# Two more input blocks through GpSimd's queue, and the last part of w turned earlier to make room for a fourth output buffer

## The chip, the cores and the metric

The kernel runs on one core of one Trainium2 chip. The metric is the device time of one execution in microseconds (us); of a kernel that was run several times the median is given. Below, DMA stands for the transfers between the chip's main memory (HBM) and the core's on-chip memory, which the core's 16 DMA engines carry out. TensorE, VectorE, ScalarE, GpSimd and SyncE are the core's engines; the profile calls them PE (with PEld for its weight loads), DVE, ACT, POOL and SP.

## The reference

For every pair of fields (i, j) with i < j, the vector of field i is multiplied by that pair's own 64 x 64 matrix, and the result is multiplied element by element with the vector of field j. There are 4096 rows, 32 fields of 64 numbers, and 496 pairs.

```python
r_inputs   # (4096, 32, 64) float32
L0_rec_W   # (496, 64, 64) float32

def _L0_rec_ref(inputs, W):
    F = inputs.shape[1]
    idx_i, idx_j = np.triu_indices(F, k=1)
    vi = inputs[:, idx_i, :]
    vj = inputs[:, idx_j, :]
    vidots = jnp.einsum('bpd,pde->bpe', vi, W)
    return vidots * vj          # (4096, 496, 64) float32
```

The input is 33.6 MB, the matrices are 8.1 MB, and the output is 520 MB.

## The kernel before

**Tiles and blocks.** The 4096 rows are cut into 16 blocks of 256 rows, and a block into 2 tiles of 128 rows, one row on each of the 128 partitions: 32 tiles, numbered 0 to 31. A block of the input is loaded as a whole (2 MB). The on-chip array `xb` has five slots of one tile each. Slots 1 to 4 hold the first two blocks; `slots_of` (line 103) says which two slots each later block takes.

**The steps.** For one tile, the work is a list of steps, each for one field i and up to 16 fields j. A step is two matmuls (line 305, the two halves of the 64 outputs), which write one PSUM tile, and an element-wise product with the fields j (line 321, VectorE), which writes the output buffer. For seven fields i (`aside`) the first step's PSUM tile is instead copied by ScalarE (line 318) and multiplied by GpSimd (line 319). Before a tile's fields can be used by TensorE, they are transposed eight at a time (`turn_x`: four transposes on TensorE, three copies on ScalarE).

**Outputs.** The steps of a tile are gathered in groups. In tiles 0 to 2 there are six groups, and these three tiles go side by side: group 0 of tiles 0, 1, 2, then group 1 of tiles 0, 1, 2, and so on. That makes 18 outputs, numbered 0 to 17 here (in places 0 to 137 of the whole order of steps; group 3 fills places 54 to 77). From tile 3 on a tile has four groups and 47 steps, and the tiles follow one another. A group fills one of three output buffers in the array `ob` (`out_home`, line 79), which SyncE then sends to HBM as one transfer of 2.3 to 4.1 MB (line 326). A buffer is written again only when its transfer has landed, that is, when all 16 DMA engines have finished their share.

**The matrices.** w is loaded in four parts (`load_w`). A part is raw at first, and must be reordered (`order_w`, line 179) and transposed (`turn_w`, line 190: 8 transposes on TensorE and a copy for each of four quarters). Parts 1 to 3 are ordered and turned in between the first steps, at the places in the list at line 248. The raw form of the last part lies at the end of `ob`, behind the three small buffers of the first three tiles.

**Reloading x.** At step 4 of tiles 3, 7, 11, 15, 19, 23 and 27, two blocks are loaded for the four tiles that come next (`loads`, line 257). A block in the list `fifteen` goes by `load_fifteen` (line 151) on GpSimd's own DMA queue, as four transfers: 120 rows, which fifteen of the DMA engines share; a tiny one (`turn_engines`) whose data nobody uses, and which moves on the engine at which the next transfer begins; and the last 8 rows in two halves, one to eight engines each. Any other block goes by `load_x` on ScalarE's queue, three steps later, as one transfer of 128 rows shared by all 16 engines. Before the change the odd block of each pair goes by GpSimd, the even one by ScalarE; of the last pair, 14 and 15, both go by GpSimd.

**What sets the order.** Each engine runs its own instructions in the program's order. The issues of GpSimd's transfers stand among its multiplies (line 319), and those of ScalarE among its copies. SyncE issues the outputs alone. Loads and outputs share the same 16 DMA engines.

Of the kernel before, what the change touches and what calls it, by code (L numbers as in the profile page):

```python
# [12 lines left out]
def kernel(  # L13
# [39 lines left out]
    LEAD = 3  # L53
    lead = [0, p0[3], p0[6], p0[9], p0[13], p0[18], NP]
    later = [0, p0[4], p0[9], p0[15] + 10, NP]
    groups = {}
# [3 lines left out]
    cap0 = max(b - a for a, b in groups[0])  # L60
    cap1 = max(b - a for a, b in groups[LEAD])
# [14 lines left out]

    def out_home(n: int, later_: bool):
        o, c = ((2 - n % 3) * cap1, cap1) if later_ else ((2 - n % 3) * cap0, cap0)  # L80
        return ob[:, o : o + c, :]

    RAW, RP = P * E2 // D, 2 * BANK // D
    assert 3 * cap0 + RAW + 2 * RP <= 3 * cap1 and LEAD * len(groups[0]) % 3 == 0

# [10 lines left out]

    fifteen = (3, 5, 7, 9, 11, 13, 14, 15)

    def slots_of(blk: int):
        e, second = divmod(blk, 2)
# [64 lines left out]
    def raw_w(c: int):  # L169
        if c + 1 < len(wrows):  # L170
            a = wrows[c + 1][0]
            return wT[:, a : a + P, :].rearrange("p r e -> p (r e)")
        return ob[:, 3 * cap1 - RAW :, :].rearrange("p r e -> p (r e)")
# [5 lines left out]
    def order_w(c: int, k: int, copy):  # L179

        r = wrows[c][1] - wrows[c][0]
        o = k * RP if c == 0 else 3 * cap1 - RAW - (1 + k % 2) * RP
        rp = ob[:, o : o + RP, :].rearrange("p r e -> p (r e)").rearrange("p (e h d) -> p e h d", h=2, d=D)
        src = raw_w(c)[:r].rearrange("p (d h e) -> p e h d", h=2, d=D)
        ins = copy(rp[:r], src[:, k * EU : (k + 1) * EU])  # L185
        if c > 0:
            tc.keep_in_program_order(ins)
        return rp
# [59 lines left out]
    for c, orders, turns in (  # L248
        (1, (2, 4, 8, 10), (4, 7, 12, 15)),
        (2, (16, 18, 26, 29), (24, 27, 32, 36)),  # L250
        (3, (56, 58, 66, 72), (62, 68, 74, 78)),
    ):
        for k in range(NU):
            due.setdefault(orders[k], []).append(("order", c, k))
            due.setdefault(turns[k], []).append(("turn", c, k))
# [15 lines left out]
    for k, copy in enumerate((v, v, v, a)):  # L271
        rps[0, k] = order_w(0, k, copy)
# [6 lines left out]
    for s, (t, st) in enumerate(sched):  # L279
# [8 lines left out]
        for what, *args in due.get(s, ()):  # L288
            if what == "x":
                xT[tuple(args)] = turn_x(*args, a)  # L290
            elif what == "turn":
                turn_w(*args, rps.pop(tuple(args)), a)
            else:
                c, k = args
                rps[c, k] = order_w(c, k, ((v, v, p, v), (v, v, p, a))[k % 2][c])
# [3 lines left out]
        if pa == base:  # L299
            ot = out_home(len(n_out), t >= LEAD)  # L300
            n_out[t, g] = ot
# [10 lines left out]
        o = pa - base  # L312
# [45 lines left out]
```

## Time and profile before

| | |
|---|---|
| median of 4 runs | 1330.44 us (1328.27 to 1330.67) |
| profiled execution: its time | 1328.27 us |
| profiled execution: its span | 1326.5 us |
| busy: TensorE / VectorE / ScalarE / GpSimd | 1138.7 / 950.2 / 471.4 / 561.9 us |
| bytes moved | 563.17 MB, mean 425 GB/s |
| read / written in HBM | 41.94 / 520.09 MB |
| output transfer of 3.8 to 4.1 MB, issue to landing | 19.5 to 20.2 us (median) |
| block by ScalarE's queue (6 of them), issue to landing | 22.6 us (median) |
| 120 rows of a block by GpSimd's queue (8 of them), issue to landing | 33.5 us (median) |

The span is the time from the first to the last instruction of the profiled execution; its device time is 1.8 us more. The slices of the page cut the span into 40 equal parts. Their row "DMA" is the busy share of the 16 DMA engines in tenths, and their row "GB/s" what was moved. In the rows of queues, q1 is SyncE's queue, q10 ScalarE's, and q0 GpSimd's, each with its packets, its MB and the time of its packets as a share of 16 engines' span. In an answer by windows a row begins with the stretch (from:to in us) and its length; then come the busy us of PE, PEld, DVE, ACT and POOL with the number of instructions, the granted clock of TensorE, the share of the DMA engines and the GB/s. A row of the timeline is: start in us, length in us, engine, line, operation, and how many instructions were merged.

The trace also has a record of every completion: a transfer adds one to its semaphore for each of the 16 DMA engines, so the sixteen times say how far apart the engines finish, though not which engine is which.

### The profile page before, as it was taken

The numbers are of one execution on the slowest core, as the hardware profiler recorded it, in microseconds if no ns is written. First come the engines' busy times: TensorE is split into PE (matmuls) and PEld (weight loads), VectorE is DVE, ScalarE is ACT, GpSimd is POOL, SyncE is SP. The second block draws the span as 40 slices with busy tenths as digits, with TensorE's granted clock in tenths as the row PEclk, the third lists the DMA queues.
The fourth block names the chain that finished last, engine by engine and source line by source line (L and its number), as shares of the span: only waits on it lengthen the run. The fifth ranks groups of instructions, "written<-read, shape, count | busy, mean of one in ns | idle before, by whom it ended". The sixth has DMA issues, their size and how long they took to land.

```text
span 1326.5 us, 17383 instructions
## 1 busy us (share of the span) xinstructions
PE 1138.7 (86%) x6644; PEld 595.4 (45%) x6644; DVE 950.2 (72%) x1287; ACT 471.4 (36%) x627; POOL 561.9 (42%) x268
## 2 busy tenths in 40 slices
PE   6989978997998978999788987889889989878883
PEld 4545544443444434444344444444444444444441
DVE  5668777784777857777677776777767777667773
ACT  4453423332333333333233332333323333333330
POOL 1862524435343444344443353443524435334440
PEclk9999989997999989999899998999989999989997
DMA  9999999999999999999999999999999999999999
GB/s 387 431 431 429 384 431 433 428 430 423 432 429 432 433 418 432 431 430 433 413 431 434 429 425 421 432 429 431 412 423 434 431 429 397 421 430 431 434 431 389
DMA packets 24658, 563.17 MB, mean 425 GB/s; under 512 B 3456, under 2 KB 3456, under 8 KB 3840
## 3 DMA queue, kind: packets, MB, share of 16 engines
q1 hardware_dynamic: 20448, 532.69, 93.9%
q0 software_dynamic: 3264, 16.80, 3.4%
q10 hardware_dynamic: 864, 12.58, 2.4%
q8 instruction: 52, 0.85, 0.2%
q14 instruction: 30, 0.25, 0.0%
HBM read 41.94 MB, written 520.09 MB: 424 GB/s over the span
## 4 chain that ended last, share of the span: by engine, by line
DMA 52%; PE 19%; DVE 10%; issue 9%; POOL 5%; ACT 3%; DVEq 0%; ACTq 0%; SPq 0%; POOLq 0%
DMA out_dram<-ob 51%; PE ps L305 17%; DVE ob L321 10%; POOL ob L319 4%; ACT ob L318 3%; PE ptx L204 1%; DMA xb<-in_r_inputs_dram 1%; POOL xb L156 0%; DVE ob L185 0%; ACT xtb L206 0%; ACT xtb L208 0%; ACT xtb L207 0%; POOL ob L185 0%; POOL scratch L148 0%; DVEq L321 0%
## 5 line engine op out<-in xcount | busy, mean ns | idle before, releaser
L321 DVE TENSOR_TENSOR ob<-ps,xb 128x1024 f32<-128x1024 f32 (+4 forms) x1277 | 940.2, 793 | 343.6 <-DMA out_dram<-ob 181.9
L305 PE MATMUL ps<-wT,xtb 64*128 64x512 f32 (+15 forms) x5760 | 1010.5, 488 | 151.3 <-DVE ob L321 76.6
L319 POOL TENSOR_TENSOR ob<-ob,xb 128x1024 f32<-128x1024 f32 x224 | 529.8, 2371 | 735.0 <-ACT ob L318 716.9
L305 PEld LDWEIGHTS ps<-wT,xtb 64*128 64x128 f32 x5760 | 504.9, 194 | 620.2 <-DVE ob L321 258.1
L318 ACT COPY ob<-ps 128x1024 f32<-128x1024 f32 x224 | 226.8, 1013 | 484.9 <-PE ps L305 307.9
L206 ACT COPY xtb<-ptx 128x512 f32<-128x512 f32 x122 | 71.5, 586 | 306.5 <-PE ptx L204 304.8
L204 PE MATMUL ptx<-ident,xb 128*128 128x128 f32 x512 | 84.8, 289 | 2.2
L204 PEld LDWEIGHTS ptx<-ident,xb 128*128 128x128 f32 x512 | 54.4, 142 | 54.3 <-issue 33.2
L208 ACT COPY xtb<-ptx 64x512 f32<-64x512 f32 x122 | 71.0, 582 | 3.0
L207 ACT COPY xtb<-ptx 64x512 f32<-64x512 f32 x122 | 70.5, 577 | 3.0
L305 PE MATMUL ps<-wT,xb 64*128 64x512 f32 (+15 forms) x244 | 41.5, 461 | 3.0 <-ACT ob L318 1.6
L305 PEld LDWEIGHTS ps<-wT,xb 64*128 64x128 f32 x244 | 20.6, 186 | 19.9 <-DVE ob L321 6.6
L195 PE MATMUL ptw<-ident,ob 128*128 128x128 f32 (+1 forms) x128 | 18.8, 299 | 10.8 <-DVE ob L185 10.2
L195 PEld LDWEIGHTS ptw<-ident,ob 128*128 128x128 f32 (+1 forms) x128 | 15.7, 158 | 15.9 <-issue 12.4
L196 ACT COPY wT<-ptw 128x1024 f32<-128x1024 f32 (+1 forms) x15 | 14.9, 992 | 9.8 <-PE ptw L195 9.8
L156 POOL DMA_DIRECT2D xb<-in_r_inputs_dram x24 | 15.2, 635 | 0.0
L185 DVE COPY ob<-wT 128x1024 f32<-128x1024 f32 (+1 forms) x7 | 7.1, 1041 | 8.8 <-DMA wT<-in_L_rec_W_dram 8.8
L148 POOL DMA_DIRECT2D scratch<-in_r_inputs_dram x10 | 9.2, 916 | 0.3 <-issue 0.3
L206 ACT COPY xb<-ptx 128x512 f32<-128x512 f32 x6 | 3.5, 588 | 13.4 <-PE ptx L204 13.3
L185 POOL COPY ob<-wT 128x1024 f32<-128x1024 f32 x4 | 7.9, 1984 | 0.0
L185 ACT COPY ob<-wT 112x1024 f32<-112x1024 f32 x1 | 2.0, 1965 | 6.7 <-DMA wT<-in_L_rec_W_dram 6.7
L185 ACT COPY ob<-ob 128x1024 f32<-128x1024 f32 x2 | 4.0, 2019 | 0.0
(11 smaller groups left out, 12.8 us busy)
## 6 DMA issues: line engine op xcount, KB each, us to landing
out_dram<-ob SPq DMA_DIRECT2D x29, 4064.0 KB, 19.5
out_dram<-ob SPq DMA_DIRECT2D x29, 4032.0 KB, 19.9
out_dram<-ob SPq DMA_DIRECT2D x29, 4000.0 KB, 20.0
out_dram<-ob SPq DMA_DIRECT2D x29, 3776.0 KB, 20.2
xb<-in_r_inputs_dram POOLq DMA_DIRECT2D x8, 1920.0 KB, 33.5
xb<-in_r_inputs_dram ACTq DMA_DIRECT2D x6, 2048.0 KB, 22.6
out_dram<-ob SPq DMA_DIRECT2D x3, 2912.0 KB, 12.6
out_dram<-ob SPq DMA_DIRECT2D x3, 2624.0 KB, 11.3
```

The lines of the kernel that those rows point to most:

```text
L156: tc.keep_in_program_order(nc.gpsimd.dma_start(out=dst[ps, :, fs], in_=rows[ps, :, fs]))
L185: ins = copy(rp[:r], src[:, k * EU : (k + 1) * EU])
L195: nc.tensor.transpose(pt[:, n, :r], rp[:r, n].rearrange("p h d -> p (h d)"), ident[:r, :r])
L196: copy(wT[:, a:b, k * EU : (k + 1) * EU], pt[:, :, :r].rearrange("p e r -> p r e"))
L204: nc.tensor.transpose(pt[:, u, :], x_tile(t)[:, f : f + 2, :].rearrange("p f d -> p (f d)"), ident)
L206: copy(xT[:, 0], pt)
L207: copy(xT[D:, 1], pt[:D])
L208: copy(xT[:D, 1], pt[D:])
L305: nc.tensor.matmul(ps[:, h, :m, :], xT[t, i // RUN][h * D : (h + 1) * D, (i + h) % 2, i % RUN // 2, :], wT[h * D : (h + 1) * D, pa : pa + ...
L318: nc.scalar.copy(dst, src)
L319: nc.gpsimd.tensor_mul(dst, dst, xj)
L321: nc.vector.tensor_mul(dst, src, xj)
```

## The change

Three edits. The blocks 6 and 10 are put into `fifteen`, so that they go by GpSimd's queue too, in four transfers; by `slots_of` their blocks and the blocks 7 and 11 take other slots. The last part of w is ordered at places 40 to 52, not 56 to 72, and turned at places 46 to 58, not 62 to 78. The memory that its raw form leaves is a fourth output buffer for the last eight of the 18 outputs of the first three tiles (from output 10 on, in place 62); the first ten go round three buffers, in another order than before. The reordered form of w's first part moves behind the first buffer.

```diff
+    FOURTH = 3 * len(groups[0]) - 8
+
     def out_home(n: int, later_: bool):
-        o, c = ((2 - n % 3) * cap1, cap1) if later_ else ((2 - n % 3) * cap0, cap0)
+        if later_:
+            o, c = (2 - n % 3) * cap1, cap1
+        elif n < FOURTH:
+            o, c = (0, 2, 1)[n % 3] * cap0, cap0
+        else:
+            k = 3 - (n - FOURTH) % 4
+            o, c = k * cap0 if k < 3 else 3 * cap1 - cap0, cap0
         return ob[:, o : o + c, :]

     RAW, RP = P * E2 // D, 2 * BANK // D
-    assert 3 * cap0 + RAW + 2 * RP <= 3 * cap1 and LEAD * len(groups[0]) % 3 == 0
+    assert 3 * cap0 + RAW + 2 * RP <= 3 * cap1 and LEAD == 3 and FOURTH % 3 == 1
...
-    fifteen = (3, 5, 7, 9, 11, 13, 14, 15)
+    fifteen = (3, 5, 6, 7, 9, 10, 11, 13, 14, 15)
...
-        o = k * RP if c == 0 else 3 * cap1 - RAW - (1 + k % 2) * RP
+        o = cap0 + k * RP if c == 0 else 3 * cap1 - RAW - (1 + k % 2) * RP
...
-        (3, (56, 58, 66, 72), (62, 68, 74, 78)),
+        (3, (40, 42, 48, 52), (46, 50, 54, 58)),
```

## The prediction

> **What bounds the kernel now.** I read the slices of the page first, then the queues, the seven places where x is reloaded, and last who was late there.
>
> Slices and queues of the page:
>
> ```profile
> DMA  9999999999999999999999999999999999999999
> GB/s 387 431 431 429 384 431 433 428 430 423 432 429 432 433 418 432 431 430 433 413 431 434 429 425 421 432 429 431 412 423 434 431 429 397 421 430 431 434 431 389
> ...
> q1 hardware_dynamic: 20448, 532.69, 93.9%
> q0 software_dynamic: 3264, 16.80, 3.4%
> q10 hardware_dynamic: 864, 12.58, 2.4%
> ```
>
> The DMA engines are never free. At the plateau of 433 GB/s the 563.17 MB take 1300.6 us of the 1326.5. So the bound is transfer, and only stretches below the plateau can be won. They are the start, the end, and the reloads. The same from windows laid over the reloads (R1 at 145 us to R7 at 1115) and one plateau (last column GB/s):
>
> ```profile
> 138.00:148.00 10.00, 9.89 (x56) 5.15 (x58) 8.86 (x12) 2.77 (x5) 5.50 (x6) 1.00 0.94 374
> 148.00:158.00 10.00, 9.93 (x65) 5.57 (x62) 8.09 (x12) 5.11 (x6) 9.73 (x5) 1.00 1.03 342
> 158.00:180.00 22.00, 15.47 (x93) 8.80 (x91) 13.01 (x20) 6.25 (x10) 4.07 (x2) 0.84 1.01 426
> 200.00:240.00 40.00, 36.93 (x216) 19.08 (x218) 31.45 (x44) 15.18 (x21) 18.08 (x8) 0.96 1.01 433
> 299.00:340.00 41.00, 31.43 (x168) 16.02 (x164) 23.85 (x33) 12.83 (x18) 17.65 (x11) 0.83 1.00 423
> 462.00:503.00 41.00, 31.88 (x178) 17.04 (x174) 24.71 (x35) 13.05 (x18) 17.90 (x11) 0.88 1.01 421
> 626.00:667.00 41.00, 31.74 (x188) 16.43 (x186) 25.74 (x38) 13.06 (x18) 17.86 (x11) 0.92 1.00 416
> 788.00:829.00 41.00, 30.24 (x178) 15.41 (x174) 24.58 (x35) 13.06 (x18) 17.69 (x11) 0.92 1.00 416
> 952.00:993.00 41.00, 32.12 (x180) 17.09 (x178) 24.68 (x36) 13.06 (x18) 17.24 (x11) 0.83 1.01 411
> 1114.00:1155.00 41.00, 35.12 (x200) 18.39 (x196) 27.52 (x40) 14.06 (x19) 21.70 (x16) 0.92 1.00 393
> ```
>
> Loss = (433 - rate)/433 x length. R1: 1.36 + 2.10 + 0.36 = 3.8 us; R2 0.95; R3 1.1; R4 1.6; R5 1.6; R6 2.1; R7 3.8. Sum 15.0 us: all that this change can touch.
>
> Why the losses grow from R2 to R7 is in the trace's completion records, sixteen increments for each transfer, one per DMA engine. On the plateau one engine ends each output transfer about 0.33 us further behind the median of the sixteen than in the transfer before. Its lag at the last output before the reload's packets is 1.5 us at R2, 4.1 (R3), 5.3 (R4), 6.4 (R5), 8.2 (R6), 6.6 (R7). A reload whose second block goes by GpSimd's queue takes some 4 to 5 us off; R7, with both blocks there, turned +6.6 into -5.3. An output buffer comes free with the last engine, so the lag delays the next output. The first engine finished an output this long before the next was issued or, positive, after it: +6.8 us ahead of R2, +4.0 (R3), +2.4 (R4), +2.8 (R5), +1.5 (R6), +1.6 (R7). I call it the backlog. When it is used up, engines hold loads alone, and those go at 250 to 300 GB/s (8 KB load packets 478 ns in R7's worst 20 us, 309 ns when mixed with outputs).
>
> Last, GpSimd in R7, where it issues both blocks as it would in R3 and R5, and in R3 as it is now:
>
> ```profile
> 1114.62 0.79 POOL L156 DMA_DIRECT2D xb<-in_r_inputs_dram  x1
> 1115.40 0.98 POOL L148 DMA_DIRECT2D scratch<-in_r_inputs_dram  x1
> 1116.38 1.87 POOL L156 DMA_DIRECT2D xb<-in_r_inputs_dram  x3
> 1118.25 0.96 POOL L148 DMA_DIRECT2D scratch<-in_r_inputs_dram  x1
> 1119.21 1.11 POOL L156 DMA_DIRECT2D xb<-in_r_inputs_dram  x2
> 1120.34 4.66 POOL L319 TENSOR_TENSOR ob<-ob,xb 128x1024 f32<-128x1024 f32 x2
> ```
>
> ```profile
> 462.89 0.79 POOL L156 DMA_DIRECT2D xb<-in_r_inputs_dram  x1
> ...
> 465.79 2.35 POOL L319 TENSOR_TENSOR ob<-ob,xb 128x1024 f32<-128x1024 f32 x1
> ```
>
> The multiply behind the issues is the last work of the tile's first output. In R3 it ends at 468.14 and SP issues the output at 468.17; in R7 the first multiply ends at 1122.7, the output goes at 1122.73.
>
> **The change part by part**
>
> *Blocks 6 and 10 leave ScalarE's queue (R3, R5).* Removed: one issue of 0.38 us on ScalarE, three steps later in the program; nobody waits for it. Added on GpSimd: four issues, 5.72 us (1114.62 to 1120.34) in place of 2.9 (462.89 to 465.79), so the multiply and the output behind it come 2.8 us later; SP has nothing else to issue meanwhile. Without a ScalarE load between them the output packets ahead also finish sooner: the output ahead of R7 ended 10.7 us after its forerunner on the first engine, that of R3 13.7, that of R5 12.4. R3: the first engine ended 6.6 us after the next issue; 6.6 - 2.8 - 3.0 = 0.8, and by the median engine 10.6 - 2.8 - 4.3 = 3.5. In R7 these were -1.6 and +0.5 for a loss of 3.8, in R6 2.9 and 5.4 for 2.1. In R7 most engines ran out of outputs, here half would. I take 2.0 us for R3, +0.9 (bounds 0 and R7's own 3.8, +2.7). R5: 4.2 - 2.8 - 1.7 + 4 (lag, below) = 3.7, nearest to R4's 4.4: loss 1.3, -0.3 (bounds -0.7 and +2.2).
>
> *Bytes for the other fifteen engines.* A block by GpSimd gives fifteen engines 16 packets of 8 KB (309 ns) and two of 4 KB (159 ns), 5.26 us; by ScalarE's queue 8 packets of 16 KB (611 ns), 4.89. Two blocks: +0.75 us. The page's queue shares, which hold the slow reloads too, give 6.0 against 5.3: +1.4 is the other end. The lagging engine finishes some 1.6 us ahead already, so what it is spared at the end is worth nothing.
>
> *The lag.* R3's pair takes off about 9.7 in place of 4.5, R5's as well, against 5.3 grown between reloads. By this count it is 4.1 at R3, near 0 at R4, 1 at R5, and ahead of the others from then on. What is late next is the spread of the other fifteen, about 2 us. The backlog then returns to R2's 6.8. R4: 1.6 to 1.0, -0.6 (0 to -0.7). R6: 2.1 to 1.0, -1.1 (0 to -1.2). R7: -1.6 + 5.2 = 3.6, its double issue stays; 3.8 to 1.4, -2.4 (0 to -2.9). The lower ends are R2's loss, the upper ends no effect.
>
> *The last part of w and the fourth buffer (R1).* Four orders (VectorE 1.03 and 1.56 us, ScalarE 2.00 and 2.04), four turns (TensorE 1.09 each, ScalarE copies 1.01 each) stand between 79.6 and 98.3 us. From 79.1 to 140 VectorE never waits for an output buffer, and TensorE is busy 9.4 to 10 of each 10 us from 80 to 120: the stage is bound by TensorE. Places 40 to 52 for orders and 46, 50 for two turns fall in the outputs at 66 to 78 us, where VectorE waited 1.4 and 1.2 us for buffers: that covers 2.2 us on TensorE; without it these outputs would slip, with a backlog of 4.5 us there. The turns at 54 and 58 stay in the bound stage. So the outputs up to the first of tile 3 come 2.2 us earlier (0 if the stage is set by other waits, 4.4 if all turns count). That first output was issued at 150.11, 2.6 us after the first engine was out of outputs (147.50); then 147.9. Its loads move up with it and stretch the output ahead. The loss of 0.6 us at 139 goes, and of the later dip about a third: -1.6 (bounds +0.5, a slip of the early outputs; and -2.8, R2's level). The fourth buffer itself allows more lead than the bound stage can use: 0. New output homes are only addresses, and the first tile-3 output still waits for the same transfer (135.84).
>
> *A rule against this change.* The trace's lag grows 0.33 us per output between 350 and 450 us, where GpSimd moves nothing. The Trainium skill, "DMA: Bandwidth & Descriptors", section "Latency and other measured facts", guesses that two slower engines are slow because of GpSimd's descriptor rings, and calls this specific to its path. By that, two more blocks there would feed the lag: R4 to R7 would keep their losses and the sum would be near 1330.5. The rows above are against it.
>
> Sum: +0.9 - 0.3 + 0.75 - 0.6 - 1.1 - 2.4 - 1.6 = -4.35 us, of a span of 1326.5 to 1322.2. The profiled execution was 1328.27, the lowest of four and 2.2 below their median; I carry the difference to the median: 1330.44 - 4.35 = **1326.1**.
>
> **Rivals**
>
> *The dips are reads beside writes, not lag.* For it: R2 loses 0.95 with hardly any lag. Against: R6 and R7 lose twice to four times as much. Then R4, R5, R6 keep theirs, R7 wins half (-1.2), R1 -1.0, R3 +0.9, bytes +0.75: -0.55, 1329.9.
>
> *Slower: the double issue on GpSimd makes R7's dip.* For it: R7 had less lag than R6 and lost 1.7 more, and its output waited for that multiply. Then R3 and R5 go to 3.8 (+2.7, +2.2), R7 stays, R4 and R6 win 1.7, R1 1.6, bytes +0.75: +2.35, 1332.8. It decides once the output behind the issues comes after the median engine has finished the one ahead (R7: 0.5 us of margin); I expect 3.5 in R3.
>
> *All at R2's level.* R1 -2.8, R4 -0.7, R5 -0.7, R6 -1.2, R7 -2.9, R3 0, bytes +0.75: -7.55, 1322.9. Against it is the double issue.
>
> **How the numbers follow.** Forecast 0.45 (own range 1324 to 1328), reads 0.25, double issue 0.17, R2's level 0.13. What a measurement of this kernel can tell from no change is about 0.2%, 2.7 us: faster below 1327.8. Faster: 0.13 + 0.40 of the forecast + 0.02 of the reads = 0.55; slower 0.15 + 0.03 of the reads = 0.18; same 0.27. The range reaches to both outer cases: 1322 to 1333.
>
> **What the changed profile would show.** Right: ScalarE's queue moves 8.39 MB and GpSimd's 20.99; R4, R6 and R7 at 420 GB/s or more; R3 near 412; the lagging engine ahead of the others at the end by some 10 us; no w order or turn after 80 us, and tile 3's first output near 148. Wrong: R6 and R7 unchanged though the lag is gone, or R3 and R5 below 400, or the early outputs late by more than 4.5 us.

## The result, and the profile after

The changed kernel takes 1332.4 us (median of 36 runs, 1329.04 to 1334.93), the kernel before 1330.2 us in the runs beside it (56 runs, 1327.94 to 1332.06). The ratio is 1.0016, with a 95% interval of 1.0011 to 1.0021: about 2 us slower, where 4.35 us less were forecast. The profiled execution took 1330.38 us, with a span of 1328.6; it is among the quicker ones of this kernel, and 2.1 us above that of before.

Slices and queues of the page of the changed kernel:

```profile
GB/s 388 434 428 433 396 432 431 431 430 427 431 430 432 430 410 427 431 429 420 423 431 432 431 422 420 425 430 429 416 424 433 429 434 403 426 432 429 431 433 352
...
q1 hardware_dynamic: 20448, 532.69, 93.9%
q0 software_dynamic: 4064, 21.00, 4.1%
q10 hardware_dynamic: 576, 8.39, 1.6%
q8 instruction: 52, 0.85, 0.2%
```

GpSimd's queue has two blocks more, ScalarE's two less, as it should be. The slice of the first reload rose from 384 to 396, that of the last from 397 to 403. The last slice of all fell from 389 to 352: 37/433 of 33.2 us, or 2.8 us, are lost there, at the end, where the prediction put nothing.

The same windows over the reloads as in the prediction, with two added right behind R3 and R5 (503 to 530 and 829 to 856 us), for the changed kernel (last column GB/s):

```profile
138.00:148.00 10.00, 9.93 (x54) 4.91 (x54) 9.09 (x11) 4.78 (x6) 8.31 (x7) 1.00 0.98 388
148.00:158.00 10.00, 6.31 (x40) 3.68 (x40) 5.27 (x9) 2.52 (x3) 5.80 (x3) 0.95 1.01 365
158.00:180.00 22.00, 20.11 (x122) 10.17 (x122) 15.23 (x25) 7.31 (x12) 5.23 (x3) 0.95 1.02 431
299.00:340.00 41.00, 31.15 (x172) 16.01 (x170) 23.33 (x34) 12.04 (x17) 16.23 (x10) 0.83 1.00 425
462.00:503.00 41.00, 33.32 (x198) 17.01 (x196) 27.68 (x40) 13.57 (x19) 20.14 (x15) 0.96 1.00 412
503.00:530.00 27.00, 19.30 (x97) 10.07 (x95) 14.16 (x18) 7.59 (x10) 13.44 (x6) 0.87 1.01 428
626.00:667.00 41.00, 30.02 (x174) 15.31 (x175) 23.55 (x35) 12.05 (x17) 15.15 (x8) 0.88 1.01 417
788.00:829.00 41.00, 32.29 (x186) 17.25 (x185) 26.50 (x37) 13.05 (x18) 18.29 (x13) 0.92 1.00 415
829.00:856.00 27.00, 20.85 (x104) 10.85 (x100) 14.56 (x19) 8.26 (x11) 13.59 (x6) 0.81 1.01 424
952.00:993.00 41.00, 28.73 (x168) 14.71 (x168) 23.09 (x34) 12.05 (x17) 14.78 (x8) 0.88 1.01 417
1114.00:1155.00 41.00, 31.20 (x184) 17.23 (x182) 25.50 (x37) 12.04 (x17) 18.68 (x13) 0.92 0.99 405
```

By the prediction's own formula the losses are now R1 2.7, R2 0.8, R3 2.0, R4 1.5, R5 1.7, R6 1.5, R7 2.7 us, 12.8 in place of 15.0. Behind R3 and R5 the two added windows had 431 and 430 GB/s before: 0.2 and 0.4 us more are lost there. So the reloads gave back 1.6 us of time, and the kernel still ended 2 us later.

The trace's completion records say how both can be. The lines below are the sixteen times at which the engines finished one output, each less their median, in us; in front stand the number of the output (by transfers: the very first output goes as two, so the last of the 135 is 134) and the time of its issue.

```
before
118  1150.0  -5.3  -0.9  -0.5  -0.4  -0.4  -0.2  -0.2  -0.0   0.0   0.0   0.1   0.2   0.3   0.3   0.3   0.8
134  1306.4  -1.6  -1.3  -1.2  -1.1  -0.6  -0.4  -0.4  -0.2   0.2   0.5   0.6   0.7   0.7   0.7   0.9   1.0
changed
118  1152.7  -3.6  -2.1  -1.4  -1.0  -0.9  -0.6  -0.4  -0.1   0.1   0.4   0.4   0.6   1.2   1.3   2.0   3.1
134  1308.5  -3.2  -1.8  -1.8  -1.1  -1.0  -0.7  -0.1  -0.1   0.1   0.4   0.5   0.5   0.6   1.6   1.9   3.8
```

Before the change the last output left the mean engine at 1324.26 us and the last one 1.08 us after it. In the changed kernel the mean engine ends at 1323.53, so 0.73 us earlier, and the last one 3.79 us behind it, at 1327.32. -0.73 + 2.71 = +2.0 us, of the 2.1 us by which the spans differ. A second profile of the changed kernel (below) has the last engine 3.88 us behind, 2.8 more than before, and the mean engine 0.4 us later than before, not earlier. In the packet records one engine works alone for the last 1.9 us: two packets of 32,256 bytes, 1.194 us each, the second behind the first, when all others have ended before the middle of the first.

That engine is not the slow one of the prediction. The slow engine shows in the packet records by its longer packets: between 350 and 450 us, before and after the change, one packet in sixteen or seventeen takes 1,207 to 1,255 ns, nearly all others 1,194; that is about 0.04 us more each, and eight such packets in an output make some 0.3 us. Followed by these packets it was 6.4 us late ahead of R7 before the change and 4.5 early behind it (output 120); in the changed kernel 3.2 late and 3.3 early, and level with the median at output 132. The engine that ends last is one of the other fifteen, and it was 3.1 us behind as R7's reload went through (output 118). The second profile shows the same with four engines, 2.9 to 4.4 us behind there and 3.5 to 4.6 at the end:

```
changed, second profile
118  1153.1  -3.7  -1.6  -0.9  -0.9  -0.7  -0.7  -0.5  -0.3   0.3   0.4   0.6   0.6   2.9   3.7   3.7   4.4
134  1309.7  -2.0  -1.8  -1.8  -0.9  -0.8  -0.6  -0.3  -0.1   0.1   1.0   1.1   1.6   3.5   4.1   4.1   4.6
```

### The profile page after: what moved, and what is told of

Same layout as the page of the kernel before. It is cut to its first block, busy times and chain, and to the rows that moved or that the text cites. A ratio compares the mean times of both kernels' runs of the same rounds, so it can differ in the third digit from the quotient of the medians.

```text
span 1328.6 us, 17395 instructions
## 1 busy us (share of the span) xinstructions
PE 1137.5 (86%) x6644; PEld 596.5 (45%) x6644; DVE 951.4 (72%) x1287; ACT 471.5 (35%) x627; POOL 566.6 (43%) x276
## 5 line engine op out<-in xcount | busy, mean ns | idle before, releaser
L165 POOL DMA_DIRECT2D xb<-in_r_inputs_dram x30 | 18.9, 633 | 0.0
```

What stands on the lines that cost most here:

```text
L165: tc.keep_in_program_order(nc.gpsimd.dma_start(out=dst[ps, :, fs], in_=rows[ps, :, fs]))
```

## The experiments

The theories change as the runs come in. Theory A: the last engine sets the end, and what a kernel leaves of the spread between the engines decides. Theory B, the prediction's own way of counting: the sum of the stretches' losses sets it, so that the loss sits in the double issue of R3 and R5. Later ones are named where they come up: the state theory is A made narrower (what counts is how R7 leaves the engines), the count theory holds the number of split blocks against it.

All times are medians; the ratios are to the kernel before on the same chip. "Split" means a block by `load_fifteen`. The last three columns come from the profiled execution of each kernel: R7's rate, by how much the last engine is behind the median at output 118, and the last output's mean engine and last engine.

| kernel | split blocks | time, us | ratio (95% interval) | R7, GB/s | last at 118 | mean end + last behind it |
|---|---|---|---|---|---|---|
| before | 8 | 1330.2 | 1 | 393 | 0.8 | 1324.3 + 1.1 |
| changed | 10 | 1332.4 | 1.0016 (1.0011 to 1.0021) | 405 | 3.1 | 1323.5 + 3.8 |
| changed, again | 10 | 1332.1 | 1.0021 (1.0012 to 1.0029) | 414 | 4.4 | 1324.7 + 3.9 |
| blocks only | 10 | 1331.36 | 1.0013 (1.0004 to 1.0021) | 418 | 3.9 | 1324.5 + 3.4 |
| w and buffer only | 8 | 1328.91 | 0.9996 (0.9987 to 1.0004) | 391 | 2.2 | 1323.6 + 1.3 |
| second block late | 10 | 1333.25 | 1.0023 (1.0012 to 1.0035) | 418 | 3.0 | 1326.1 + 3.3 |
| 6 and 10 whole | 8 | 1329.22 | 0.9994 (0.9985 to 1.0003) | 396 | 1.0 | 1323.7 + 1.2 |
| 6 and 10 whole, again | 8 | 1329.97 | 1.0003 (0.9994 to 1.0013) | 390 | 1.0 | 1323.8 + 1.4 |

**The two parts alone.** The first run has only the edit of `fifteen`, the second only the other two edits.

```diff
-    fifteen = (3, 5, 7, 9, 11, 13, 14, 15)
+    fifteen = (3, 5, 6, 7, 9, 10, 11, 13, 14, 15)
```

> Of the three edits only blocks 6 and 10 by GpSimd's queue; w and the output buffers as before. The profile after the change gave, against before: R1 to R7 lost 2.2 us less in all, but the last engine ended 3.8 us behind the median of the sixteen at the last output, where before it was 1.0. Theory A (the end is set by the one engine that is last; what the reloads save on the average engine is given back in a wider spread at the end): +3 us against before, and a spread of 3 to 4 us at the end. Theory B (the double issue on GpSimd, which holds up a multiply and the output behind it, is the whole cost): R3 and R5 lose about 1 us more each, +1.5 us, spread at the end as before. If the whole +2.2 us lies in the early w and the buffers: within 0.5 us of before.

```diff
+    FOURTH = 3 * len(groups[0]) - 8
...
+        elif n < FOURTH:
+            o, c = (0, 2, 1)[n % 3] * cap0, cap0
...
-        (3, (56, 58, 66, 72), (62, 68, 74, 78)),
+        (3, (40, 42, 48, 52), (46, 50, 54, 58)),
```

> Only the early w and the fourth buffer; blocks 6 and 10 by ScalarE's queue as before. Both theories: the loss at R1 falls from 3.8 us to about 2.7, as in the changed kernel, R2 to R7 as before, spread at the end about 1 us: -1.1 us (0 to -1.6). If this part is what made the change slower: +1 us or more, with the first outputs of group 3 late.

The blocks alone cost 0.13%, the early w and the fourth buffer by themselves can't be told from no change (0.04% less). So the loss comes with the two blocks. The first run doesn't decide between the theories: its 1.5 us are theory B's figure, and R3 and R5 did fall, to 407 and 409 GB/s; the spread at the end is theory A's. Where the blocks are split, the last engine ends 3.4 us behind the mean; without them 1.3.

**Is it the double issue on GpSimd?** The second block of a pair was issued three steps later, behind the multiply that the output waits for.

```diff
-            for b in (loads[s], loads[s] + 1):
-                if b in fifteen:
-                    load_fifteen(b)
+            load_fifteen(loads[s] + (loads[s] not in fifteen))
+        if s - 3 in loads and loads[s - 3] in fifteen:
+            load_fifteen(loads[s - 3] + 1)
```

> The changed kernel, but where both blocks of a reload go by GpSimd (R3, R5, R7), the second is issued three steps later, behind the multiply that the double issue held up. Theory B: the output behind it goes 2.8 us earlier, R3, R5 and R7 come back to 418 GB/s or more from 412, 415 and 405, and the time falls 2.5 us against the changed kernel. Theory A: the rates come back as well, but the time falls by less than 1 us, since the last engine's lag of 3.8 us at the end stays or grows.

R3's output goes at 468.0 us again, as before the change (468.2; 469.8 with the double issue), and the time does not follow: 1333.25. What the second issue costs the multiply is not what makes the kernel slower. The rates say less: R3 has 420 GB/s, R7 418 and R5 414, but the changed kernel's own second profile has 422, 414 and 414 there, with the double issue in place:

```profile
462.00:503.00 41.00, 30.90 (x188) 16.63 (x186) 26.23 (x38) 12.72 (x19) 19.30 (x14) 0.96 1.00 422
1114.00:1155.00 41.00, 32.92 (x182) 17.58 (x180) 24.87 (x37) 12.04 (x17) 18.87 (x13) 0.88 1.00 414
```

**Is it GpSimd's queue, or the split?** Blocks 6 and 10 stay on GpSimd's queue, but as one transfer of 128 rows over all sixteen engines.

```diff
-                if b in fifteen:
+                if b in (6, 10):
+                    tc.keep_in_program_order(load_x(b, nc.gpsimd))
+                elif b in fifteen:
                     load_fifteen(b)
```

> The changed kernel, but blocks 6 and 10 go by GpSimd's queue as one transfer of 128 rows shared by all sixteen engines, so that no engine is spared. Theory A: the lagging engine is not relieved twice, so the lag ahead of R6 and R7 is back at 6 to 8 us, and the end moves by 1 us or more either way, with another spread at the end than 3.8. Theory B: one issue instead of four (0.8 us in place of 2.8), R3 and R5 lose 1 us less in all; -1 to -1.5 us against the changed kernel.

Windows over R3 to R7 of this kernel:

```profile
462.00:503.00 41.00, 32.73 (x192) 16.63 (x190) 26.58 (x38) 13.33 (x19) 17.64 (x11) 0.96 1.01 426
626.00:667.00 41.00, 31.15 (x176) 16.38 (x176) 23.82 (x35) 12.04 (x17) 15.24 (x9) 0.88 1.01 416
788.00:829.00 41.00, 32.50 (x188) 17.59 (x186) 26.26 (x38) 13.05 (x18) 17.89 (x12) 0.92 1.00 416
952.00:993.00 41.00, 30.90 (x174) 15.96 (x175) 24.05 (x35) 12.04 (x17) 15.19 (x8) 0.88 1.00 416
1114.00:1155.00 41.00, 33.10 (x200) 16.53 (x198) 27.52 (x39) 13.88 (x19) 21.80 (x16) 1.00 1.01 396
```

This run answers two questions. First, the time is back (1329.22, and 1329.97 in a second run, below), so it is the splitting of these blocks and not the queue that costs some 2 to 3 us. (The one issue in place of four is not it: R3's output goes at 468.0 us here as in the run before, which stayed slow.) Second, the slow engine is late again ahead of the reloads, by 4.9 (R4), 5.5 (R5), 6.0 us (R6) against 2.3, 2.9 and 2.5 in the changed kernel, and yet R4, R5 and R6 run at 416 here against 417, 415 and 417 there. In the second profile of the changed kernel the slow engine is level with the median ahead of R4 and R6 and 0.5 us late ahead of R5, at 414, 414 and 416 GB/s. Lags near 0, of 2.5 and of 5 to 6 us go with the same rates, 414 to 417: the prediction's cause of these losses was wrong.

**A wait in R7.** R7 is where before the change the engines ran out of outputs, and where fifteen of them came out within 1.7 us of each other (output 118). If that is what keeps the end together, a wait put into R7 of the changed kernel should pay. Three multiplies of a small tile were put behind R7's issues, in the changed kernel and in the one before.

```diff
+            if loads[s] == NBLK - 2:
+                for _ in range(3):
+                    tc.keep_in_program_order(nc.gpsimd.tensor_mul(idle, idle, idle))
```

> The changed kernel with three multiplies of a 128x512 tile by itself put on GpSimd behind the issues of blocks 14 and 15 (R7); by its row of 2.33 us for 128x1024 they take about 3.5 us, and the first output of that stretch goes that much later. Theory A (the end is set by the last engine, and the wait for the late engines in R7 is what levels them in the kernel before): in R7 the engines run out of outputs as before, its rate falls from 405 to about 393 GB/s (a loss of 1.1 us more), and the last engine ends about 1 us behind the median in place of 3.8: 1331 us, not slower than the changed kernel (1329.5 to 1332.4). Theory B (the end follows the sum of the losses in the stretches, the engines' spread is a side matter): the added wait is added to the time, 1333.5 to 1336 us.

> The same three multiplies in the kernel before, at the same place. Its engines already run dry in R7 and end within 1 us of one another, so there is no spread left to win: both theories expect the whole wait on top, 1332.5 to 1334 us, and R7 near 370 GB/s. It is the control for the run with the same wait in the changed kernel: if that gains or stays and this loses about 3 us, the difference is the levelling.

GpSimd's row of instructions in the changed kernel with the wait:

```profile
1119.07 1.10 POOL L168 DMA_DIRECT2D xb<-in_r_inputs_dram  x2
1120.20 1.05 POOL L300 TENSOR_TENSOR idle<-idle 128x512 f32<-128x512 f32 x1
1121.20 2.35 POOL L334 TENSOR_TENSOR ob<-ob,xb 128x1024 f32<-128x1024 f32 x1
1123.50 1.04 POOL L300 TENSOR_TENSOR idle<-idle 128x512 f32<-128x512 f32 x1
```

The three came out one between every two multiplies, so only 1.05 us of the 3.1 stands ahead of the output. Times 1331.63 (ratio 1.0014, 1.0006 to 1.0023) and 1330.12 (0.9999, 0.9990 to 1.0008): neither moved, and the control's 1332.5 was missed as well. R7 of the changed kernel stayed at 414 GB/s, so nothing was levelled and the theories were not tested. A microsecond of wait in R7 cost nothing that these runs can tell; their intervals are about 1.2 us wide to either side.

A longer wait followed, two copies of 128x1024 ahead of that one multiply; and the same in the changed kernel without block 10.

```diff
+            if held < 0 and s >= max(loads):
+                held = s
+                for _ in range(2):
+                    nc.gpsimd.tensor_copy(dst, dst)
             nc.gpsimd.tensor_mul(dst, dst, xj)
```

> The changed kernel with two copies of 128x1024 on GpSimd ahead of the multiply that the first output of R7 waits for; by the 1.98 us of the copies of w they hold this output about 4 us, where the earlier wait came out as 1.05 us only. Theory A (a wait in which nearly all engines run out of outputs levels them): the median engine ends the output ahead 3.4 - 4 = 0.6 us before this one is issued, as in the kernel before; the last engine then ends 1 to 1.5 us behind the median in place of 3.8, the mean engine 1 to 2 us later; the time stays or falls by up to 1.5 us against the changed kernel. Theory B (sum of the losses): 3 to 4 us more than the changed kernel. Theory C (blocks by fifteen engines put one engine behind by themselves, levelled or not): the last engine stays 3 to 4 us behind and the time is 2 us more.

> The same two copies in the changed kernel with block 10 in ScalarE's queue, whose mean engine ended earliest of all (1323.0 us of the profile) with the last 3.3 us behind it. Theory A: the levelling wins 2 us of these 3.3 and costs 1 to 2 us of the mean: 1328 to 1329 us. Theory B: 1331 to 1333.

Both lost far more than any theory said: 1338.24 (1.0063) and 1336.23 (1.0055). The output behind the copies was issued at 1129.7 and 1126.4 us in place of 1121.2. That is 8.5 and 5.2 us later, not 4: in GpSimd's row the copies take 1.05 and 1.03 us, but a multiply of 2.35 us stands between them, and the next one waits 1.9 and 1.5 us for ScalarE's copy. R7 fell to 362 and 373 GB/s:

```profile
1114.00:1155.00 41.00, 26.43 (x130) 13.17 (x126) 16.32 (x21) 11.30 (x15) 23.18 (x17) 0.81 1.00 362
1155.00:1200.00 45.00, 38.34 (x228) 21.52 (x228) 35.00 (x47) 14.07 (x19) 16.48 (x7) 0.87 0.93 398
```

The first of them ends the mean engine at 1333.5 us, against 1324.7 for the changed kernel on that chip. But its records are the clearest of the study, because R7 now ends with all sixteen engines level:

```
118  1170.9  -0.1  -0.1  -0.0  -0.0  -0.0  -0.0  -0.0  -0.0   0.0   0.0   0.0   0.0   0.1   0.1   0.1   0.2
121  1195.5  -0.1  -0.1  -0.1  -0.1  -0.0  -0.0  -0.0  -0.0   0.0   0.0   0.0   0.1   1.0   1.2   1.9   2.1
127  1249.1  -0.2  -0.1  -0.1  -0.1  -0.1  -0.1  -0.0  -0.0   0.0   0.4   0.5   1.5   1.6   1.6   1.8   3.0
134  1317.8  -0.6  -0.6  -0.5  -0.5  -0.5  -0.5  -0.4  -0.3   0.3   0.6   0.7   0.7   0.8   1.1   1.3   3.9
```

The last engine ends 3.9 us behind the median again, but this time it is the slow one: it goes from 1.2 at output 121 to 4.0 at 131, about 0.3 us per output. A dry spell that levels all sixteen also takes away the slow engine's lead. What the kernel before has after R7 ends better: fifteen engines level, and the slow one 5 us ahead, which it uses up by the end.

**R7 with one split block.** Block 14 went to ScalarE's queue, once in the kernel before and once in the changed one.

```diff
-    fifteen = (3, 5, 7, 9, 11, 13, 14, 15)
+    fifteen = (3, 5, 7, 9, 11, 13, 15)
```

> The kernel before with block 14 by ScalarE's queue, so that R7 is built like R4 and R6. Theory A: R7 loses less (near 412 GB/s, 1.8 us won), but its engines do not all wait, so the slow one starts the last eighteen outputs some 3 us behind and falls 0.33 us further with each: it ends 6 to 9 us behind the median, 1333 to 1337 us. Theory B: R7 wins 1.8 us and the other engines move 0.4 us less: about 1328 us.

```diff
-    fifteen = (3, 5, 6, 7, 9, 10, 11, 13, 14, 15)
+    fifteen = (3, 5, 6, 7, 9, 10, 11, 13, 15)
```

> The changed kernel with block 14 back in ScalarE's queue: nine blocks by fifteen engines too, but one only in R7. State theory: R7 near 415, no levelling, and the slow engine gets 5 us of lead less for the last eighteen outputs: last engine 4 to 7 us behind the mean, 1332 to 1335 us. Count theory: as the other kernels with nine, 1329 to 1330.

In the kernel before: 1334.4 us (1.0031, 1.0020 to 1.0042). R7 and two outputs of this run:

```profile
1114.00:1155.00 41.00, 31.29 (x176) 16.04 (x172) 25.61 (x34) 12.85 (x19) 19.29 (x11) 0.92 1.01 416
```

```
118  1156.4  -0.8  -0.8  -0.5  -0.4  -0.3  -0.3  -0.3  -0.1   0.1   0.1   0.2   0.5   0.5   0.9   1.0   4.3
134  1312.3  -0.1  -0.1  -0.1  -0.1  -0.1  -0.0  -0.0  -0.0   0.0   0.1   0.3   0.4   0.4   0.7   1.6   8.2
```

R7 runs at 416 GB/s instead of 393, 2.2 us better, and the mean engine ends no later (1324.2); the slow engine starts the last outputs 4 us behind and ends 7.5 behind the mean. The rate of the stretch went up and the time went up with it. So the sum of the stretches' losses is not the time. In the changed kernel: 1332.07 us (1.0008, 0.9999 to 1.0017), last engine 5.3 us behind the mean, again the slow one. Both are as the theory that the last engine decides had them.

**One block less, one more, and where.** Each split block in turn.

```diff
-    fifteen = (3, 5, 6, 7, 9, 10, 11, 13, 14, 15)
+    fifteen = (3, 5, 6, 7, 9, 11, 13, 14, 15)            # without 10
+    fifteen = (3, 5, 7, 9, 10, 11, 13, 14, 15)           # without 6
+    fifteen = (3, 5, 6, 7, 9, 10, 11, 12, 13, 14, 15)    # and 12
```

> The changed kernel with block 10 back in ScalarE's queue: one block more by fifteen engines than before, not two. Theory A: the time goes by whether R7 still levels the engines. With lag ahead of R7 between the 6.6 us of before and the 3.4 of the changed kernel it does so in part: last engine 2 to 3 us behind at the end, 1330.5 to 1332 us. Theory B: half of the difference that blocks 6 and 10 made, 1331.

> The changed kernel with block 6 back in ScalarE's queue and block 10 by fifteen engines: the counterpart of the run without block 10, which lost nothing against the kernel before. If what costs is the tenth block (the count), this also comes out near 1329 us; if it is block 10 (R5 with its double issue, nearer to R7), near 1332 us. Theory A with the count: last engine about 3 us behind the mean at the end, mean engine near 1323.

> The changed kernel itself, on the chip and beside the runs of the kernel before that the other three have: 1331.5 to 1333 us, ratio 1.0016, and in the profile the last engine 3 to 5 us behind the mean at the end, whichever engine it is.

> The changed kernel with block 12 (R6) by fifteen engines as well: eleven. State theory: R7 at 410 or more, not levelled, last engine 3 to 4 us behind, 1332 to 1334 us, much like ten. Count theory: 2 to 3.5 us more than ten, 1334 to 1336, and the first engine further ahead at the end.

Without 10: 1328.83 (0.9993, 0.9984 to 1.0002), below what either theory said (1330.5 to 1332). Without 6: 1330.34 (1.0002, 0.9993 to 1.0011). The changed kernel on that chip: 1332.1, as before. In their profiles the last engine ends 3.3, 4.0 and 3.9 us behind the mean; the mean ends at 1323.0, 1323.3 and 1324.7. So neither block costs much alone, and the pair costs 2 to 3 us. With 12 as well: 1338.41 (1.0060, 1.0048 to 1.0073), more than either theory said, but this run doesn't measure the count. Block 12's two slots lie side by side, so its transfer has packets of another size, and from R6 on the engine that is spared is no longer the slow one: that one was 4.1 us late ahead of R7, 5.4 late behind it (output 122), and 7.9 at the end.

In the next two the split blocks stand earlier; what is taken out goes as one whole transfer on GpSimd's queue.

```diff
-                if b in fifteen:
+                if b in fifteen and b not in (13,):         # second run: (11, 13)
                     load_fifteen(b)
+                elif b in fifteen:
+                    tc.keep_in_program_order(load_x(b, nc.gpsimd))
```

> The changed kernel with block 13 (R6) loaded by GpSimd as one transfer over all sixteen engines: nine blocks by fifteen engines, as in the two runs without block 10 and without block 6, but none between R5 and R7. State theory (the spread at the end is small only where R7 finds the slow engine 5 us or more late, so that the others run dry and are levelled, and both of R7's blocks spare it): lag ahead of R7 about 8 us, R7 below 400 GB/s, last engine 1 to 1.5 us behind the mean at the end, 1328 to 1329.5 us. Count theory (what costs is each block by fifteen engines beyond nine, wherever it stands): 1329 to 1330, and no more levelled than the other two kernels with nine.

> The changed kernel with blocks 11 and 13 as whole transfers: eight blocks by fifteen engines as before the change, but early ones, and R7's pair. State theory: the lag grows through R5 and R6 to 10 us or more ahead of R7; R6 and R7 below 405 and 390, the last engine 1 to 1.5 us behind at the end, the mean 1 to 2 us later: 1329 to 1331 us. Count theory: eight as before, 1329 to 1330.

With 13 whole: 1331.76 (1.0010, 1.0001 to 1.0018), where both theories said 1330 or less. The slow engine came to R7 3.7 us late, not 8. R7 did run dry (395 GB/s) and did level the engines in part: at output 131 the last was 2.1 us behind. Then one engine lost 2 us between two outputs, and ended 4.0 behind. In the packet records, near 1301 us, stand a load of the program itself, 16 KB (0.88 us), and, around it, two output packets of 1.77 and 1.60 us that otherwise take 1.19. With 11 and 13 whole: 1329.89 (0.9997, 0.9988 to 1.0006), inside both ranges. The rest of the state theory's forecast missed: the slow engine came 6.8 us late, not 10, R6 ran at 422 GB/s, and the last engine ended 4.2 us behind. The profiled execution was the slowest of eleven, and there one engine lost 1.2 and 0.8 us in steps at outputs 118 and 120.

**Again.** Two kernels a second time, as tests of chance; their edits are above.

> The changed kernel with block 10 in ScalarE's queue a second time, beside the kernel before on one chip: its first runs gave 0.9993 of the kernel before with an interval that held 1. If leaving block 10 unsplit is a gain in itself, it repeats at 0.999 to 0.9997 (1328.5 to 1329.6 us); if that was the chance of where the spread of the engines fell, it lands at 1.000 to 1.0015 like the other three kernels with nine split blocks.

> The changed kernel with blocks 6 and 10 as whole transfers of GpSimd's queue a second time. The state theory expects the fifteen engines levelled in R7 again, the last engine 1 to 1.5 us behind the mean at the end, and 0.999 to 0.9998 of the kernel before (1328.7 to 1329.8 us); if the end was small by chance, 3 to 4 us behind and 1331.

Without 10: 1330.46 (0.9998, 0.9990 to 1.0007); the gain of the first time did not repeat. In this profile R7 ran at 397 GB/s (412 the first time), the last engine was 2.2 us behind the median at output 118, and it ended 3.9 us behind the mean: at output 131 it had lost 1.7 us, beside a program load of 0.89 us at 1297.9 us. Six and ten whole: 1329.97 (1.0003, 0.9994 to 1.0013), which misses the 0.9998 asked for, while the levelled end repeated in the profiled execution, the quickest of its twelve: 1.4 us behind the mean, and a last slice like that of the kernel before, as its row of slices shows (R7's slice 386, the last 386):

```profile
GB/s 387 431 428 430 400 429 433 431 430 426 431 431 432 430 421 428 429 428 422 417 433 432 431 424 424 431 429 429 416 427 431 430 431 386 421 431 432 433 430 386
```

**What they show together.** The end is the mean engine's end plus the distance of the last engine from it; that holds by definition, and what the profiles add is the distance. It is 1.1 to 1.4 us in five profiles (before, before with the wait, w and buffer only, 6 and 10 whole twice), and 3.3 to 7.5 us in all others. In the five, R7 falls to 388 to 396 GB/s, and both its blocks spare a slow engine that comes 6 to 8 us late. Three more are near to this (13 whole, 395 GB/s, the slow engine 3.7 us late; 11 and 13 whole, 393 and 6.8; without 10, again, 397 and 4.4), and were thrown back to 4.0, 4.2 and 3.9 by steps of one engine. The three kernels that were profiled twice came out alike both times (3.8 and 3.9 changed, 3.3 and 3.9 without 10, 1.2 and 1.4 with 6 and 10 whole). By the number of split blocks the ratios are 0.9994 to 1.0003 with eight (R7's pair among them), 0.9993 to 1.0010 with nine, 1.0013 to 1.0023 with ten (the long wait apart). That splitting 6 and 10 both makes the kernel some 2 us slower is shown; that it does so by keeping R7 from levelling the other fifteen engines fits the profiles, but the one kernel built to undo just that (the long wait) undid too much, and the state theory missed the time of one kernel with nine (13 whole). Nor is the distance alone the time: the kernels without 10 and without 6 end 3.3 to 4.0 us behind the mean and are as quick as the kernel before, in two of their three profiles with a mean engine 0.9 to 1.3 us earlier. Why the tenth block costs more than the ninth stays open. No kernel here is faster than the one before by more than its interval.

## Why the prediction was wrong

The steps, as the prediction put them:

| step | forecast, us | measured, us |
|---|---|---|
| R1, early w and fourth buffer | -1.6 | 3.8 to 2.7: -1.1 |
| R2 | 0 | -0.2 |
| R3, double issue | +0.9 | +0.85, and 0.2 behind it |
| R4, lag | -0.6 | -0.1 |
| R5 | -0.3 | +0.1, and 0.4 behind it |
| R6, lag | -1.1 | -0.6 |
| R7, lag | -2.4 | -1.1 |
| bytes on the fifteen | +0.75 | not seen by itself |
| the end | 0 | +2.7 |

The measured column is one profile against one. The second profile of the changed kernel gives, by the same windows, R1 -1.3, R2 +0.1, R3 -0.1 and 0.6 behind it, R4 +0.2, R5 +0.2 and 0.5 behind it, R6 -0.5, R7 -2.0, and the end +2.8. Single stretches move by up to 1 us between two profiles of one kernel; the end is the same in both.

**The end: the step that failed.** "The lagging engine finishes some 1.6 us ahead already, so what it is spared at the end is worth nothing" was right in kind about that engine (followed by its long packets it is about 0.7 us early at the end; the one 1.6 us early is another) and was taken as the whole of the end. The sum then treats a stretch's GB/s as time. GB/s is a sum over sixteen engines, so it gives the time of the mean engine, and that came 0.73 us earlier in the profile shown and 0.4 us later in the second. (Against the -1.6 measured at the reloads 0.9 us are missing in the first; the forecast had 0.75 for the bytes on the fifteen, and no run shows that term by itself. In the second profile the reloads won 2.3 us and the mean engine still ended later: there the plateau from 1200 to 1300 us, which the sum takes as fixed, ran at 429 GB/s and not 433, 0.9 us; the rest was not traced.) The kernel waits for the last engine, and its distance went from 1.1 to 3.8 us. No rival priced this either. The prediction had the line that held it, R7's lag that "turned +6.6 into -5.3", and read it as a cost of R7; it did not ask where the other fifteen stood afterwards, or what else the dry spell did.

**The lag: cause and size wrong.** "Why the losses grow from R2 to R7" was put down to the slow engine. With blocks 6 and 10 whole the lag is twice as long and R4 to R6 lose the same. So the terms for R4 and R6 had no ground, and what R7 won is half of what was forecast in the first profile: its first engine finished 0.2 us after the next issue (2.2 in the second profile), where 3.6 was forecast. The size failed too: "R3's pair takes off about 9.7" was taken from R7. Followed by its long packets, the slow engine went from 3.5 us late to 0.9 early over R3's pair (outputs 49 to 55), 4.4 us, and about 3 over R5's; in the second profile R3's pair took off some 4 us as well. It did not run "ahead of the others from then on", and at the end it is level with the median in one profile and 1.3 us late in the other (output 132), not 10 us ahead. Why a pair takes off 11 us in R7 of the kernel before and 4 in R3 was not found.

**R3, right in its mechanism; R5, wrong in sign.** GpSimd in R3 of the changed kernel:

```profile
461.73 0.79 POOL L165 DMA_DIRECT2D xb<-in_r_inputs_dram  x1
462.51 0.98 POOL L157 DMA_DIRECT2D scratch<-in_r_inputs_dram  x1
463.49 1.87 POOL L165 DMA_DIRECT2D xb<-in_r_inputs_dram  x3
465.36 0.97 POOL L157 DMA_DIRECT2D scratch<-in_r_inputs_dram  x1
466.32 1.11 POOL L165 DMA_DIRECT2D xb<-in_r_inputs_dram  x2
467.45 4.67 POOL L328 TENSOR_TENSOR ob<-ob,xb 128x1024 f32<-128x1024 f32 x2
```

5.72 us from the first issue to the multiply, as forecast, and the output at 469.84 with the first engine 1.35 us and the median engine 4.31 us from done (forecast 0.8 and 3.5). That the rate came out at the 412 of the forecast is luck: the second profile has 422 in R3, with 3.2 and 5.5 us left, and 422 behind it. The 2.0 us taken for R3 also stood below R6's 2.1, though less was left than in R6. R5 had 2.9 and 5.2 us left, and lost 0.1 more in its window and 0.4 behind it, since the lag relief it counted on was worth nothing. Its 1.3 us were not read off the rows rightly either: with 4.4 us left R4 lost 1.6, so 3.7 should have given no less, and the term no gain.

**R1, right in its mechanism.** Orders and turns of the last part end at 83 us (80 forecast). The first output of tile 3 is issued at 147.24 (forecast 147.9), and R1 won 1.1 of 1.6 us. The first engine is out of outputs 0.3 us before that issue, where it was 2.6 us.

**The rule weighed.** The Trainium skill, "DMA: Bandwidth & Descriptors", section "Latency and other measured facts", guesses that two engines are slower because of GpSimd's descriptor rings. With 25% more data on GpSimd's queue the slow engine loses some 0.33 us per output as before, there is one such engine, and its packets are long where GpSimd moves nothing: the rule's cause is not seen here. Its sum, 1330.5, was nearer to the result than the forecast, but R6 and R7, which by it keep their losses, won 0.6 and 1.1 us.

**The rivals.** "Reads beside writes, not lag" had the stretches of the first profile almost right: R4 and R5 unmoved, R7 -1.2 (measured -1.1), R1 -1.0 (-1.1), R3 +0.9 (+1.0 with what is lost behind it); it too ended at the mean engine. "The double issue on GpSimd makes R7's dip", the slower one, gave 1332.8, next to what was measured (1332.4), for a reason that did not hold: R3 did not fall to the 393 GB/s of R7, and freeing the multiply won nothing.

## What to carry to other kernels

In a kernel bound by its transfers, price an edit twice: by the mean of the DMA engines (the GB/s of the stretches) and by the last of them. The completion records give the distance between the two; look at it behind the last stretch that mixes loads and outputs, and at the end. A dip in the rate can be worth keeping: if most engines wait there for a late one, it may be the place where they come level again, and an edit that fills the dip can carry their spread to the end. That reading fits the profiles here; it was not proved. Relief for one slow engine is worth what it can use by the end, no more.

## What the runs showed of the hardware that was not expected

- One of the sixteen DMA engines is slower while the program runs: its 32,256-byte packets take 1,207 to 1,255 ns against 1,194, in stretches without any GpSimd transfer, in every profile of this study. It is not slower for good: the last output goes when the compute engines have finished, and in none of the 20 profiles does one of its 128 packets take more than 1,211 ns. What lengthens them before stays open.
- The program's own loads are seen in the spread. There are 52 of 16 KB in the changed kernel's page (the row q8 instruction), one about every 25 us, each on one engine for 0.96 us on average (0.88 to 1.09). With all engines level (the long wait, output 118) they can be followed: from 1191 to 1307 us there are six, and each time the output packet before the load is 0.57 to 0.62 us longer than usual and the one behind it 0.37 to 0.41, so that with the load itself the engine loses 1.9 us. In the kernel before, behind R7, only the packet behind the load is longer, and a load costs its engine 1.3 to 1.4 us. Where such a step meets the engine that is last already, as with 13 whole and without 10 the second time, it goes into the time; it may be part of why the changed kernel's runs lie 5.9 us apart and those of the kernel before 4.1, which no run here tests.
- A rise of R7 from 393 to 416 GB/s came with 4 us more (block 14 by ScalarE's queue, in the kernel before).
- The Trainium skill says on the page "DMA: Bandwidth & Descriptors", in "SWDGE vs HWDGE vs iDMA", of another kind of traffic and in a paragraph marked unconfirmed, that a bulk load runs at the pace of its slowest engine. This kernel's end shows the same for its outputs, with 1.1 to 7.5 us between the mean engine and the last.
